# Two graph layers in fp32: the order of the pieces on all engines and on the load queue, written anew

## The chip, the cores and the metric

The kernel runs on one core of a Trainium2 chip. The metric is the time of one execution on the device in microseconds (us); the median of several executions is compared.

## The reference

`x` holds 128 graphs of 128 nodes with 512 features, in fp32. `adj` is one 128 x 128 adjacency matrix for all of them. Two layers follow each other, each with a residual and a layer norm:

```python
# layer 0: attention with 8 heads of 64, masked by adj
q = (x @ Wq + bq).reshape(b, n, H, HD)      # k, v alike
scores = jnp.einsum('bqhd,bkhd->bhqk', q, k) / jnp.sqrt(jnp.float32(HD))
scores = scores + (1.0 - adj)[None, None, :, :] * -1000000000.0
attn = jax.nn.softmax(scores, axis=-1)
out = jnp.einsum('bhqk,bkhd->bqhd', attn, v).reshape(b, n, d)
x = _layernorm(x + out @ Wo + bo)
# layer 1: graph attention, and beta times the node's own product
h = jnp.einsum('bnc,cf->bnf', x, W)
s1 = jnp.einsum('bnf,f->bn', h, a1); s2 = jnp.einsum('bnf,f->bn', h, a2)
e = jax.nn.leaky_relu(s1[:, :, None] + s2[:, None, :], negative_slope=0.2)
e = e * mask[None, :, :]                    # mask is adj
att = jax.nn.softmax(e, axis=2)
x = _layernorm(x + jax.nn.elu(jnp.einsum('bij,bjf->bif', att, h) + beta * h))
```

## The kernel before

**Tiling.** A group is two graphs (64 groups). Each of the five products with a 512 x 512 weight (q, k, v, w for Wo, h for W) is done in 2 x 2 blocks with seven block products instead of eight: some factors are differences of weight blocks (`weight_sum`, made once at the start) or of blocks of the activations (`block_sum`, on GpSimd, POOL). `product` (L318, L325) issues the matmuls of one of the seven; the products of q and k run over two groups at once, those of v, w and h over one. `take_part` (L369, L372, L375) takes a sum out of PSUM and `add_block` (L383, VectorE, DVE) adds a second one to it. The running sums stay in PSUM: `main` and `two` from product 1 or 2 on, `side` from product 7 on, all from one pool of eight banks.

**What happens to a graph.** The blocks of x come in by four DMAs (`load_blocks`, L86), DVE turns them (`turn_x`, L248), POOL makes the block sums. After q and k: `scores` (matmuls psc, L397, two banks), `mask` (DVE, L405, two halves), `row_max` (L413), `exps` (ScalarE, ACT, L419), `row_inv` (L426), `normalise` (ACT, L433). The normalised weights must be transposed in blocks of 32: `attn_write` sends them to DRAM (SP, L440), `attn_read` brings them back block by block with four DMAs (SP, L445), and `turn_attn` turns the blocks on DVE (L462, two halves). Then `attend` (matmuls po, L472), `attend_evict` (ACT, L484), the product w, statistics, and the second layer: row products (L523), logits, softmax (L612 to L641), the weights of which take the same way through DRAM (`weights_write` L587, `weights_read` L594, `weights_turn` L600), `aggregate` (matmuls pz, L660), the product h, ELU (L671 to L680), layer norm and `store` (L750). The tile of raw x for the residual comes in by `fetch_x` (L96).

**What sets the order.** Nothing schedules at run time or at build time: every piece of this work stands in a list with a place, a number in us that is only used to sort. `rows(g)` gives the places for an even and an odd group, `last_rows(g)` those of the last two groups, and a table `other` replaces them for groups 0 to 5 and the groups 58 to 61. `lay(g)` adds `(g // 2) * STEP` to each place, so two groups (four graphs) make one step. About 40 `at(...)` lines place the weight sums and loads. All pieces are sorted by place, and each is issued when its turn comes; so this one order is also the order of instructions on PE (TensorE), DVE, ACT and POOL and of the DMAs on SP, which takes most loads and stores. An engine works strictly in that order, and SP too: a DMA that must wait holds those behind it.

In the steady step of the kernel before, the pieces around the attention of an even group have these places:

```python
(20.282, attn_write, b0), (26.115, attn_read, b0), (28.151, attn_write, b1),
(31.844, turn_attn, b0, 0), (32.855, attn_read, b1), (34.286, turn_attn, b0, 1),
(34.906, turn_attn, b1, 0), (35.094, turn_attn, b1, 1),
(35.392, attend, b0), (35.411, attend, b1),
```

Between the places 28.151 and 32.855 the odd group's two `fetch_x` (29.459 and 31.350) and the `fetch_blocks` of the odd group of the next step (−41.301 in its own step, so 31.323 here) stand on the same queue.

Of the kernel before, what the change touches and what calls it, by code (L numbers as in the profile page):

```python
# [13 lines left out]
P = 128  # L14
# [4 lines left out]
STEP = 72.624  # L19
# [3 lines left out]
def gnn_two_layers(  # L23
# [40 lines left out]
    G = 2  # L64
# [155 lines left out]
    def weight_sum(name, n, eng):  # L220
        w_sb = W_SB[name]
        a11, a21 = w_sb[:, :2, :HF], w_sb[:, :2, HF:]
        a12, a22 = w_sb[:, 2:, :HF], w_sb[:, 2:, HF:]
        if name not in sums:
            sums[name] = cpool.tile([P, 3, G, HF], F32, tag=f"s_{name}", name=f"s_{name}")
        s2, s3, s4 = (sums[name][:, i] for i in range(3))
        if n == 3:
            eng.tensor_tensor(s3, a11, a21, ALU.subtract)
        elif n == 1:
            eng.tensor_tensor(a21, a21, a22, ALU.add)  # L230
        elif n == 2:
            eng.tensor_tensor(s2, a21, a11, ALU.subtract)
        else:
            eng.tensor_tensor(s4, a12, s2, ALU.subtract)
        left[name] = {1: a11, 2: a12, 3: s4, 4: a22, 5: a21, 6: s2, 7: s3}


    right, tx, qT, kT, vb, y, hp, main, side, oT, zT, xr = ({} for _ in range(12))
# [20 lines left out]

    def block_sum(name, g, n):  # L260

        if name == "x":
            b11, b12, b21, b22, (t1, t2, t3, t4) = x_blocks(g % 2)
        else:
            src = oT if name == "w" else zT
            b11, b12 = src[g * G][:, :2], src[g * G + 1][:, :2]
            b21, b22 = src[g * G][:, 2:], src[g * G + 1][:, 2:]
            if (name, g) not in tx:
                tx[name, g] = grp.tile(
                    [P, 4, 2, N], F32, tag=f"t{name}", name=f"t{name}_{g}", bufs=1  # L270
                )
            t1, t2, t3, t4 = (tx[name, g][:, i] for i in range(4))
        to, a, b = {1: (t1, b12, b11), 2: (t2, b22, t1), 3: (t3, b22, b12), 4: (t4, b21, t2)}[n]
        nc.gpsimd.tensor_tensor(to, a, b, ALU.subtract)  # L274
        if name != "x":
            right[name, g] = {1: b11, 2: b21, 3: b22, 4: t4, 5: t1, 6: t2, 7: t3}

    def factor(name, g, n):

        if name in "qkv":  # L280
            b11, b12, b21, b22, (t1, t2, t3, t4) = x_blocks(g % 2 if name == "v" else None)
            return {1: b11, 2: b21, 3: b22, 4: t4, 5: t1, 6: t2, 7: t3}[n]
        if (name, g) in right:
            return right[name, g][n]

        src = oT if name == "w" else zT
        return {1: src[g * G][:, :2], 2: src[g * G][:, 2:]}[n]
# [114 lines left out]
    def mask(b, j):  # L402
        if j == 0:
            s_t[b] = wk2.tile([P, H, N], F32, tag="s", name=f"s_{b}")
# [10 lines left out]
    def exps(b, k):  # L415
        if k == 0:
            rsum[b] = st.tile([P, H], F32, tag="rsum", name=f"rsum_{b}")
# [10 lines left out]
    def normalise(b, k):  # L428

        if k == 0:  # L430
# [27 lines left out]
    def turn_attn(b, half):  # L458
        if half == 0:
# [305 lines left out]
    def rows(g):  # L765

        b0, b1 = g * G, g * G + 1
        if g % 2 == 0:
            return (
                (-63.18, fetch_blocks, g), (-56.066, turn_x, g, 0), (-50.12, turn_x, g, 1),  # L770
                (-32.921, block_sum, "x", g, 3), (-31.465, block_sum, "x", g, 1),
                (-28.542, product, "q", g, 1), (-28.403, take_part, "q", g, 1, 0, 0),
                (-26.676, product, "k", g, 1), (-26.003, product, "k", g, 2),
                (-24.525, product, "q", g, 7), (-23.847, product, "q", g, 2),
                (-22.29, take_part, "k", g, 1, 0, 0), (-22.016, add_block, "q", g, 2, 0, 0),
                (-20.3, block_sum, "x", g, 2), (-19.926, product, "q", g, 6),
                (-17.572, add_block, "k", g, 2, 0, 0), (-16.877, take_part, "q", g, 6, 1, 0),
                (-16.095, fetch_x, b1), (-13.558, product, "k", g, 6), (-12.431, product, "q", g, 5),
                (-11.287, take_part, "k", g, 6, 1, 0), (-11.187, take_part, "q", g, 5, 1, 1),
                (-10.474, product, "k", g, 7), (-9.901, fetch_x, b0), (-9.327, product, "k", g, 5),  # L780
                (-7.731, take_part, "k", g, 5, 1, 1), (-7.172, block_sum, "x", g, 4),
                (-7.022, product, "q", g, 3), (-6.693, add_block, "q", g, 7, 1, 1),
                (-3.761, product, "q", g, 4), (-3.502, add_block, "k", g, 7, 1, 1),
                (-2.536, product, "k", g, 3), (-2.35, product, "k", g, 4),
                (-1.976, add_block, "q", g, 4, 1, 0), (0.256, take_part, "k", g, 3, 0, 1),
                (0.285, take_part, "q", g, 3, 0, 1), (0.542, add_block, "k", g, 4, 1, 0),
                (1.258, scores, b0), (1.278, scores, b1), (2.004, residual, b1),
                (3.445, product, "v", g, 1), (3.721, mask, b0, 0), (4.631, mask, b0, 1),
                (4.957, row_max, b0), (5.077, take_part, "v", g, 1, 0, 0),
                (5.333, product, "v", g, 6), (5.333, exps, b0, 0), (5.499, residual, b0),  # L790
                (6.069, product, "v", g, 7), (6.116, exps, b0, 1), (6.127, mask, b1, 0),
                (6.728, take_part, "v", g, 6, 1, 0), (7.139, exps, b0, 2), (8.211, exps, b0, 3),
                (8.411, product, "v", g, 5), (10.448, mask, b1, 1),
                (11.898, take_part, "v", g, 5, 1, 1), (12.291, row_inv, b0),
                (12.598, normalise, b0, 0), (12.926, product, "v", g, 2), (13.642, normalise, b0, 1),
                (14.582, add_block, "v", g, 7, 1, 1), (14.95, normalise, b0, 2),
                (15.194, row_max, b1), (15.197, normalise, b0, 3), (16.817, exps, b1, 0),
                (17.265, product, "v", g, 4), (17.509, exps, b1, 1),
                (18.686, add_block, "v", g, 2, 0, 0), (19.881, product, "v", g, 3),
                (19.881, exps, b1, 2), (20.282, attn_write, b0), (20.467, exps, b1, 3),  # L800
                (22.18, row_inv, b1), (22.328, add_block, "v", g, 4, 1, 0),
                (22.702, normalise, b1, 0), (22.86, normalise, b1, 1), (26.083, normalise, b1, 2),
                (26.115, attn_read, b0), (26.457, normalise, b1, 3), (28.151, attn_write, b1),
                (29.815, take_part, "v", g, 3, 0, 1), (31.844, turn_attn, b0, 0),
                (32.855, attn_read, b1), (34.286, turn_attn, b0, 1), (34.906, turn_attn, b1, 0),
                (35.094, turn_attn, b1, 1), (35.392, attend, b0), (35.411, attend, b1),
                (38.896, attend_evict, b0), (38.952, attend_evict, b1), (39.488, product, "w", g, 1),
                (40.642, block_sum, "w", g, 1), (44.25, take_part, "w", g, 1, 0, 0),
                (45.185, block_sum, "w", g, 2), (48.299, product, "w", g, 6),
                (48.643, take_part, "w", g, 6, 1, 0), (48.916, block_sum, "w", g, 3),  # L810
                (50.753, product, "w", g, 2), (51.619, product, "w", g, 5),
                (51.848, product, "w", g, 7), (52.53, take_part, "w", g, 5, 1, 1),
                (52.885, block_sum, "w", g, 4), (53.606, add_block, "w", g, 2, 0, 0),
                (54.759, add_block, "w", g, 7, 1, 1), (54.917, product, "w", g, 3),
                (55.177, take_part, "w", g, 3, 0, 1), (55.873, product, "w", g, 4),
                (55.948, bn_stats, y, b1, "c"), (59.19, add_block, "w", g, 4, 1, 0),
                (59.58, row_product, b1, 0), (59.651, bn_aggr, b1, "c"),
                (59.978, bn_stats, y, b0, "c"), (60.733, bn_aggr, b0, "c"),
                (61.568, row_product, b1, 1), (62.033, add_eps, g, "c"), (62.533, inv_std, g, "c"),
                (63.073, row_product, b0, 0), (63.654, row_product, b0, 1), (64.313, scale_s, g),  # L820
                (64.596, s2_turn, g), (65.373, s2_write, g), (66.603, norm_c, b0),
                (72.522, norm_c, b1), (72.851, s2_read, g), (73.73, edge, g, 0),
                (74.467, edge, g, 1), (74.643, leaky, g), (74.812, edge_max, g),
                (77.496, edge_exp, g), (79.435, edge_inv, g), (80.677, weights, g, 0),
# [492 lines left out]
```

## Time and profile before

| | |
|---|---|
| time, median of 3 runs | 2369.22 us (2368.44 to 2373.42) |
| span of the profiled execution | 2365.3 us, TensorE clock 0.998 |
| ACT busy | 1494.1 us (63%) |
| POOL busy | 874.8 us (37%) |
| DMA | 269.31 MB, mean 114 GB/s |

A profile is of one execution; its span runs from the first to the last instruction. Here it is 3.9 us below the median of the runs. A line of a group or of the timeline reads: start or busy us, engine, line, operation, output tile <- input tiles, count, and in brackets the idle time of the engine ahead of it with what ended it. SPq is the queue of SP's own instructions, which issue DMAs; the number beside such a line is the time that issuing took, not the transfer.

The chain of waits, followed back from the last instruction, is made of these engines:

```profile
PE 86%; DMA 6%; DVE 3%; SPq 3%; issue 1%; ACT 1%; DVEq 0%; ACTq 0%; POOLq 0%; POOL 0%
```

### The profile page before, as it was taken

How to read it: one execution, taken by the hardware profiler on the slowest of the kernel's cores; microseconds unless marked ns; L12 is line 12 of the kernel's file. 1: busy time of each engine (PE TensorE's matmuls, PEld its weight loads, DVE VectorE, ACT ScalarE, POOL GpSimd, SP SyncE). 2: the span in 40 equal slices, each digit the busy share in tenths (PEclk: the TensorE clock that was granted, in tenths of full speed). 3: DMA queues.
4: the chain of work that ended last, by engine and by line, in shares of the span. 5: the costliest groups of instructions: out<-in, count | busy, mean ns of one | idle time of the engine just before them, and what ended most of it. 6: DMA issues, size and time to landing. Idle time of an engine off the chain costs nothing.

```text
span 2365.3 us, 42947 instructions
## 1 busy us (share of the span) xinstructions
PE 2332.2 (99%) x14129; PEld 2045.5 (86%) x14129; DVE 1923.8 (81%) x4198; ACT 1494.1 (63%) x5251; POOL 874.8 (37%) x1044
## 2 busy tenths in 40 slices
PE   9999999999999999999999999999999999999997
PEld 8888888888888888888888888888888888888885
DVE  7778887888887888878888887888788887888887
ACT  4565665766756666667566576665666666756665
POOL 6333333343333343433333333333334343333331
PEclk9999999999999999999999999999999999999999
DMA  5433434334334343343343443433434434344332
GB/s 184 123 94 110 128 91 127 109 103 134 97 112 131 99 117 119 97 132 101 111 133 91 120 124 94 130 114 94 136 97 114 124 96 128 101 112 135 92 125 76
DMA packets 255942, 269.31 MB, mean 114 GB/s; under 512 B 57356, under 2 KB 204568, under 8 KB 255336
## 3 DMA queue, kind: packets, MB, share of 16 engines
q1 hardware_dynamic: 254160, 265.06, 38.3%
q8 instruction: 112, 1.84, 0.3%
q14 instruction: 110, 0.90, 0.1%
q10 hardware_dynamic: 1256, 0.66, 0.1%
q0 software_dynamic: 304, 0.85, 0.1%
HBM read 157.62 MB, written 108.85 MB: 113 GB/s over the span
## 4 chain that ended last, share of the span: by engine, by line
PE 86%; DMA 6%; DVE 3%; SPq 3%; issue 1%; ACT 1%; DVEq 0%; ACTq 0%; POOLq 0%; POOL 0%
PE p1w L318 12%; PE p1q L325 9%; PE p1k L325 9%; PE p1v L318 9%; PE p1h L318 8%; PE psc L397 5%; PE pz L660 5%; PE p7q L325 5%; PE p7k L325 5%; DMA ab<-scr 5%; PE p7w L318 4%; PE po L472 4%; PE p7v L318 4%; PE p7h L318 3%; PE p2q L325 2%; PE p2k L325 2%
## 5 line engine op out<-in xcount | busy, mean ns | idle before, releaser
L419 ACT ACTIVATE s<-s,nmax 128x128 f32<-128x128 f32 x1024 | 397.1, 392 | 109.0 <-DVE nmax L413 109.0
L433 ACT ACTIVATE sb<-s,rinv 128x128 f32<-128x128 f32 x1024 | 323.0, 394 | 1.4 <-DMA scr<-sb 1.3
L484 ACT ACTIVATE oT<-po,bias_c 128x128 f32<-128x128 f32 x512 | 145.9, 380 | 222.6 <-PE po L472 222.1
L375 ACT ACTIVATE kT<-p1k,bias_c 128x256 f32<-128x256 f32 x256 | 106.2, 466 | 182.9 <-PE p1k L325 182.9
L372 DVE TENSOR_TENSOR w<-p1w,x 128x256 f32<-128x256 f32 x252 | 105.9, 420 | 140.9 <-PE p1w L318 140.6
L453 POOL TENSOR_TENSOR x<-x,bo_b_in 128x512 f32<-128x512 f32 x128 | 175.6, 1373 | 71.5 <-DMA x<-in_x_dram 71.1
L405 DVE SCALAR_TENSOR_TENSOR s<-psc,amask 128x512 f32<-128x512 f32 x256 | 165.7, 670 | 41.8 <-PE psc L397 40.1
L462 DVE STREAM_TRANSPOSE attnT<-ab 128x512 f32<-128x512 f32 x256 | 169.7, 691 | 34.2 <-DMA ab<-scr 34.2
L419 ACT ACTIVATION_READ_ACCUMULATOR s<-s,nmax 128x1 f32 x1024 | 195.3, 191 | 0.0
L369 ACT COPY h<-p1h 128x256 f32<-128x256 f32 x252 | 94.5, 375 | 157.8 <-PE p1h L318 151.8
L523 DVE SCALAR_TENSOR_TENSOR ya<-w,wa_row 128x512 f32<-128x512 f32 x256 | 191.8, 749 | 2.3
L274 POOL TENSOR_TENSOR tx<-xT 128x256 f32<-128x256 f32 x128 | 92.4, 734 | 188.4 <-DVE xT L248 164.0
L413 DVE TENSOR_REDUCE nmax<-s 128x8 f32<-128x1024 f32 x128 | 155.6, 1216 | 2.3
L274 POOL TENSOR_TENSOR th<-zT 128x256 f32<-128x256 f32 x63 | 46.1, 731 | 273.3 <-ACT zT L667 273.3
L248 DVE STREAM_TRANSPOSE xT<-xblk 128x512 f32<-128x512 f32 x128 | 141.9, 1110 | 5.4 <-DMA xblk<-in_x_dram 5.3
L472 PEld LDWEIGHTS po<-attnT,v 128*64 128x64 f32 x2048 | 109.8, 137 | 38.2 <-DVE attnT L462 15.9
L472 PE MATMUL po<-attnT,v 128*64 128x128 f32 x2048 | 132.3, 277 | 10.1 <-DVE attnT L462 9.9
L660 PEld LDWEIGHTS pz<-attT,x 128*128 128x128 f32 x1024 | 130.5, 193 | 9.8 <-issue 4.9
L369 ACT COPY v<-p1v 128x256 f32<-128x256 f32 x256 | 91.7, 371 | 70.2 <-PE p1v L318 66.1
L660 PE MATMUL pz<-attT,x 128*128 128x128 f32 x1024 | 131.5, 277 | 4.1 <-DVE attT L600 2.7
L318 PE MATMUL p1v<-wv_sb,xT 128*128 128x256 f32 x512 | 133.9, 385 | 0.0
L318 PE MATMUL p1w<-wo_sb,oT 128*128 128x256 f32 x504 | 132.5, 385 | 0.0
(681 smaller groups left out, 6153.3 us busy)
## 6 DMA issues: line engine op xcount, KB each, us to landing
scr<-sb SPq DMA_DIRECT2D x128, 512.0 KB
ab<-scr SPq DMA_DIRECT2D x512, 128.0 KB
x<-in_x_dram SPq DMA_DIRECT2D x128, 256.0 KB
out_dram<-u SPq DMA_DIRECT2D x127, 256.0 KB
xblk<-in_x_dram SPq DMA_DIRECT2D x252, 128.0 KB
pb<-s2d SPq DMA_DIRECT2D x62, 128.0 KB
attd<-att SPq DMA_DIRECT2D x62, 128.0 KB
ab<-attd SPq DMA_DIRECT2D x248, 32.0 KB
```

Source lines behind the costliest of these rows:

```text
L318: nc.tensor.matmul(out, b[:, c, :], a[:, c, :], start=first and c == 0, stop=(c == 1), skip_group_check=True,)
L325: nc.tensor.matmul(out[:, m, :], a[:, c, m * P : (m + 1) * P], b[:, c, :], start=first and m == 0 and c == 0, stop=(c == 1), skip_group_ch ...
L369: nc.scalar.copy(dst, src)
L405: nc.vector.scalar_tensor_tensor(s_t[b][:, j * HP : (j + 1) * HP, :], psc[b][j], SCALE, amask.rearrange("p (o n) -> p o n", o=1).broadcast ...
L413: nc.vector.tensor_reduce(nmax[b], s_t[b], AX.X, ALU.max, negate=True)
L419: nc.scalar.activation(s_t[b][:, h, :], s_t[b][:, h, :], AF.Exp, bias=nmax[b][:, h : h + 1], accum_out=rsum[b][:, h : h + 1],)
L433: nc.scalar.mul(sb[b][:, :, h, :], s_t[b][:, h, :].rearrange("p (b c) -> p b c", c=Q), rinv[b][:, h : h + 1],)
L453: nc.gpsimd.tensor_tensor(xr[b], xr[b], later["bo"], ALU.add)
L462: nc.vector.transpose(attnT[b].rearrange("p h (a r) -> p a h r", r=Q)[:, rows], ab[b].rearrange("p a (h c) -> p a h c", c=Q)[:, rows],)
L472: nc.tensor.matmul(po[b][j * HD : (j + 1) * HD, m, :], vb[b][:, h * HD : (h + 1) * HD], attnT[b][:, j * HP + m, :], start=True, stop=True,)
L523: nc.vector.scalar_tensor_tensor(z, y[b], 1.0, wa_row[j], ALU.mult, ALU.mult, accum_out=s12[g][:, i, j : j + 1])
L660: nc.tensor.matmul(pz[b][:, c, :], x1[b][:, c * P : (c + 1) * P], attT[g][:, i, :], start=True, stop=True,)
```

## The change

All places are new, and `STEP` is 72.19 instead of 72.624. So that any order can be written, three helpers no longer depend on which part comes first: the factors of a product are named by `part` before their block sums are issued, `left` is filled at the head of `weight_sum`, and a tile is allocated by whichever half or part comes first. The number of instructions on each engine, the arithmetic and the tiles are the same.

```diff
-STEP = 72.624
+STEP = 72.19
...
+    def part(name, g, k):
+        i = int(k[1]) - 1
+        if name in "qkvx":
+            b11, b12, b21, b22, t = x_blocks(None if name in "qk" else g % 2)
+            return t[i] if k[0] == "t" else {"b11": b11, "b12": b12, "b21": b21, "b22": b22}[k]
+        if k[0] == "b":
+            src = (oT if name == "w" else zT)[g * G + int(k[2]) - 1]
+            return src[:, 2 * i : 2 * i + 2]
+        if (name, g) not in tx:
+            tx[name, g] = grp.tile([P, 4, 2, N], F32, tag=f"t{name}", name=f"t{name}_{g}", bufs=1)
+        return tx[name, g][:, i]
...
     def factor(name, g, n):
...
+        return part(name, g, ("b11", "b21", "b22", "t4", "t1", "t2", "t3")[n - 1])
...
     def mask(b, j):
-        if j == 0:
+        if b not in s_t:
...
```

The places that matter for the text below, even group, before and after (b0, b1 are its two graphs):

| piece | before | after |
|---|---|---|
| scores b0, b1 | 1.258, 1.278 | 3.373, 2.413 |
| exps b1, first to last | 16.817 to 20.467 | 14.370 to 17.078 |
| attn_write b0, attn_read b0 | 20.282, 26.115 | 14.498, 17.153 |
| attn_write b1 | 28.151 | 20.928 |
| fetch_blocks, fetch_x of other groups between them | yes | no |
| attn_read b1 | 32.855 | 23.583 |
| turn_attn b0, b1 (the earlier half) | 31.844, 34.906 | 23.333, 29.930 |
| attend b0, b1 | 35.392, 35.411 | 32.389, 33.269 |
| product v, 1 and 2 | 3.445, 12.926 | −44.207, −41.618 |

For the odd group of a step:

| piece | before | after |
|---|---|---|
| scores b0, b1 | 35.432, 35.452 | 4.333, 34.289 |
| attn_read b1 | 69.49 | 63.183 |
| turn_attn b1, the earlier half | 71.946 | 67.674 |
| attend b0, b1 | 73.841, 73.861 | 72.703, 73.583 |

At the start, the five constant loads of `load_later` (adjacency, beta, bo, the two halves of a; on POOL's queue) are issued before the first block sums instead of after six of them; the adjacency's even before the operation that makes the identity matrix. TensorE begins with the products 2 and 1 of q and then of k, which need no differences, where it began with 1 and 7 of q. At the end the scores of graphs 126 and 127 stand earlier among the products, in the matmuls' order by some 10 and 5 us.

## The prediction

> **What bounds the kernel now.** I read the page's busy shares first, then the waits of TensorE, then the line of the attention transpose, then one step in the timeline on three engines.
>
> ```profile
> PE 2332.2 (99%) x14129; PEld 2045.5 (86%) x14129; DVE 1923.8 (81%) x4198; ACT 1494.1 (63%) x5251; POOL 874.8 (37%) x1044
> ```
>
> TensorE (PE) is busy for 99% of the span, and the change takes no matmul away. So only gaps between matmuls can be won. The waits of PE say which:
>
> ```profile
> PE po L472 <- DVE attnT L462: 9.9, 18, 1.2
> PE pz L660 <- DVE attT L600: 2.7, 1, 2.7
> PE early L145 <- DMA bias_rows<-in_L_gnn_bv_dram: 2.0, 1, 2.0
> ...
> PE pz L660 <- DVE vec_('c',60)_22068 L512: 1.4, 1, 1.4
> PE p1v L318 <- DVE v L383: 1.2, 1, 1.2
> ```
>
> Total us, times, longest. One wait repeats, the attention product (po) on the transposed weights (attnT); the others happen once, at the start or the end. The line of the transpose itself, L462, says what it waits for and who waits for it:
>
> ```profile
>   DMA ab<-scr: 34.2, 32
> who waited for it (us, times):
>   PEld po L472: 15.9, 25
>   PE po L472: 9.9, 18
> ```
>
> The 32 times are one per step of four graphs. A stalled step, seen on SP (the load queue), DVE and PE:
>
> ```profile
> 1987.81 0.42 SPq L440 DMA_DIRECT2D scr<-sb  x1
> 1990.79 1.75 SPq L445 DMA_DIRECT2D ab<-scr  x4
> 1995.93 0.34 SPq L440 DMA_DIRECT2D scr<-sb  x1
> 1996.70 0.35 SPq L96 DMA_DIRECT2D x<-in_x_dram  x1
> 1997.16 1.98 SPq L86 DMA_DIRECT2D xblk<-in_x_dram  x4
> 1999.25 0.39 SPq L96 DMA_DIRECT2D x<-in_x_dram  x1
> 1999.74 2.97 SPq L445 DMA_DIRECT2D ab<-scr  x4
> ```
>
> ```profile
> 2007.13 1.31 DVE L462 STREAM_TRANSPOSE attnT<-ab 128x512 f32<-128x512 f32 x2 [1.95 <-DMA ab<-scr]
> ```
>
> ```profile
> 2008.49 1.09 PE L472 MATMUL po<-attnT,v 128*64 128x128 f32 x16 [1.15 <-DVE attnT L462]
> ```
>
> The first graph's scores go to DRAM at 1987.81 and are read back from 1990.79. The second graph's are written at 1995.93, but six transfers of the next input stand between its write and its read (1996.70 to 1999.25). The data is there at 2007.13, DVE idle for 1.95 us before it, and PE loses 1.15 us.
>
> What can be won at most: a step holds 14 products of q and k at 1.728 us start to start, 42 of v, w and h at 0.864, and po 3.80, scores 3.98, pz 3.56, together 71.8 us. The best steps take 72.18 (score starts at 883.04 and 955.22 in the timeline), because the small matmuls cost some 0.4 us at their borders, in both orders. The mean of 26 steps is (2210.37 − 319.99) / 26 = 72.71 (starts of pz). So about 0.53 us a step is stall. The span, 2365.3, is 2305.5 us of matmuls at their own spacing, 8.2 before the first product beyond the warm-up's, 2.0 in the first scores (to 66.7), 26.1 to 2226.7 (29.7 steps: 11.3 of borders, about 15 of stalls), 13.4 from there to PE's end at 2355.2, and 10.1 of tail.
>
> **What the Trainium skill says.** "DMA: Bandwidth & Descriptors", section "Queues, rings and completion order": each DMA engine consumes one queue's descriptors in ring order, and goes round between queues packet by packet. The trace agrees: in the step of 1054.74 the 512-byte packets of xblk moved until 1056.3, and the read's 1024-byte packets only from 1057.2 to 1059.8; the first graph's read, issued at 1045.77 with nothing ahead of it, moved from 1046.9 to 1049.2. Its section "Anatomy of one DMA" gives some 2 us of fixed cost, most of it waiting for the write's receipt; here write to read issue is 2.98 us (1987.81 to 1990.79), so that stays in the chain. "TensorE: Matmul & The Clock Gate", "What's actually happening": after an idle window of about 3.4 us the clock halves. One place agrees: after the 2.7 us wait at 2315.98 two pz take 3.48 us, elsewhere 1.78.
>
> **The change, part by part.** No instruction is added or dropped on any engine; all is order.
>
> *Steady step, queue.* Between the second write and read nothing is left on SP (the blocks and x are issued after the read or elsewhere in the step). That removes 1999.74 − 1996.70, about 3.0 us, and the read's data no longer lies behind xblk's packets: about 3.7 us from issue to landing instead of 6.2, 2.5 us more.
>
> *Steady step, compute.* The second graph's scores now come first on PE, and its masks close up. Counted from the start of its scores with before's durations: scores, both masks (0.6 each), maximum (1.14) and the first graph's 8 exponentials (0.39 each) end at 9.9, its 8 normalise (0.30 each) with copies at 13.2, the second's exponentials at 16.6, reciprocal and normalise at 19.6, write 19.7, read 22.6, data 26.5, two transposes of 0.65 end at 27.8. PE's order puts the second attention product at about 31.2. So 3.4 us of cover. If the read were as slow as now (6.2), the end is 30.4 to 31.0 and 0.2 is left. The stall goes in both cases; what is late next is the third score block in a row (below), the ACT copies of h before two products (cover 1.3) and the transposed weights of the second layer (1.4), each off the path by that much. I cost them at nothing, but leave 0.07 us a step for chance meetings of transfers, 2 us in all: **−13 us** of the 15. Range −15 (all) to −4 (copies take 0.35 a step back).
>
> *Moved work.* The v products of the even graphs start a step earlier; their two running sums hold one PSUM bank of eight for 53 planned us (places −44.2 to 8.9; before 3.4 to 19.9). Score blocks need two banks each, and three of them in a row (before: two) make six. This takes no time while DVE empties banks in time: a mask takes 0.6 us, a score block 1.0, and what is ahead of the masks on DVE leaves 1.3 us. Cost 0, bounds 0 to 1.2 a step.
>
> *Start.* POOL issues the five constant loads first (before: at 12.62 to 15.44). They take 0.71 + 0.54 × 2 + 1.06 = 2.85 us of POOL, only the first of them (0.71) ahead of ident, which the warm-up at 1.48 waits for; it ends at 8.1 now and would end at 8.8, still before the first product at 10.21. But their 0.85 MB (queue 0) now run beside wq and xblk, in a stretch where the DMA is full (412 GB/s from 7.00 to 10.20). If they take their whole share, wq comes 0.85 / 0.412 = 2.1 us later, if none, 0: I take +1.2. The stalls at 43.70 (1.24) and 45.97 (0.3) are gone, as the v products no longer wait there: −1.5. The four products that start need 6.9 us, against 7.05 of weight differences and block sums behind wq: +0.2. Sum **0**, bounds ±1.5.
>
> *End.* pz of group 61 waits 2.71 us and then 1.7 us at half clock. DVE was the chain there: adds, maximum and statistics queue ahead of the transpose. The scores of graph 126 move up by 10 us, those of 127 by 5, so their masks and one maximum are out of this stretch; I count 7.4 us of DVE behind the weights where PE leaves 7.0, so 0.5 of the wait stays, without the half clock: −3.9. PE's order behind it is the same, and DVE, which caught up in that pause, now reaches attnT of 126 (0.7) and the spread of the second logits (1.0) late: +1.4 to +1.7. Tail unchanged (10.1). Sum **−2.5**, bounds −6 to +1.
>
> Sum: −13 + 0 − 2.5 = −15.5; the profiled execution goes from 2365.3 to 2349.8. The median of the runs stands 3.9 above that execution (2369.22), so 2353.7; I say 2353.5. A measurement can tell some 0.2%, 4.7 us, from no change.
>
> **Rivals.**
> - *Forecast, steady stalls gone:* 2353.5, own range 2346 to 2361. Chance 0.60.
> - *The stall moves on:* the next late thing (ACT's copies of h, or the transposed weights) takes back 0.35 us a step: −15.5 + 10 = −5.5, 2363.7. For it: ACT's queue is denser around them. Against: covers of 1.3 us and more. Chance 0.16; nearly half of it lies within 0.2%.
> - *The ends are worse:* constants delay wq by 2.1, pz keeps its wait and half clock: −15.5 + 2 + 5 = −8.5, 2360.7. Speaking for it: PE's order at the end is nearly the same. Chance 0.10.
> - *Slower, score blocks waiting for banks:* three in a row with a bank held make PE wait for DVE's masks in each step. If DVE is late by its cover and another block, the price is 1.2 us a step, 31 × 1.2 = 37: 2369.2 − 15.5 + 37 = 2391. From 0.5 us a step it eats the gain (15.5 / 31). For it: PE is 99% busy, so nothing hides such a wait, and DVE at 81% is the next engine. Against: the waits of before show no score block waiting for DVE beyond "issue". Chance 0.14.
>
> Faster by over 0.2%: 0.60 + 0.09 + 0.09 = 0.78; within: 0.07 + 0.01 = 0.08; slower: 0.14. Range 2344 to 2369: it takes in the bounds of the three sums (−15 −1.5 −6 gives 2346.7; a little is left below for borders) and the two rivals that stay faster, and leaves out the slower one.
>
> **What would show it.** Right: the row "po <- attnT" of PE's waits falls from 9.9 to under 2 us; DVE's idle before the transpose under "ab<-scr" nearly goes; mean step 72.2 to 72.3 (pz start to pz start); on SP the second read follows its write by about 3 us; pz of group 61 waits under 1 us with the clock full after it. Wrong: a new repeated wait of PE of 0.3 us or more a step, with psc or p1h as the waiting group, or a first product later than 12.5 us.

## The result and the profile after

| | before | after |
|---|---|---|
| median of the runs | 2370.01 us (2368.44 to 2373.42, 4 runs) | 2394.78 us (2393.06 to 2395.28, 4 runs) |
| span of the profiled execution | 2365.3 us | 2393.4 us |

The ratio after to before is 1.0101, 95% interval 1.0087 to 1.0115: the change makes the kernel slower by 1.0%. TensorE's clock is 0.998 in both.

The page of after, busy time of the engines and the chain that ended last:

```profile
PE 2350.2 (98%) x14129; PEld 2044.6 (85%) x14129; DVE 1945.4 (81%) x4198; ACT 1482.8 (62%) x5251; POOL 875.6 (37%) x1044
...
PE 43%; DVE 17%; ACT 11%; DMA 8%; issue 3%; SPq 2%; POOL 0%; DVEq 0%; POOLq 0%
```

The chain was PE for 86% before and is PE for 43% now; DVE and ACT have 28% of it. Something outside PE paces the kernel, though PE is still busy for 98% of the span. The tile view of the transposed weights (attnT) says that the old stall is gone:

```profile
  DMA ab<-scr: 2.8, 4
...
who waited for it (us, times):
  ACT oT L480: 33.0, 37
```

DVE's idle before this transpose fell from 34.2 to 2.8 us, and PE is no longer among those who wait for it. The waits of PE in after (total us, times, longest) show what came instead:

```profile
PE p1h L314 <- ACT h L365: 13.1, 28, 1.3
PE early L145 <- DMA bias_rows<-in_L_gnn_bv_dram: 5.2, 1, 5.2
```

A product of h waits for ACT to copy a finished sum of h out of PSUM (L365, `take_part`), 28 times. The mean step, from one p2q to the next over 23 steps, is 73.30 us; it was 72.71.

**Where the 28.1 us between the two spans lie.** I put PE's matmuls on an axis of their own spacing, as the prediction did: each takes there the time that such a matmul has from its start to the next one's when nothing is waited for. Then I subtracted that axis from the true starts. What remains is PE's loss, here by stretch of the axis, in us, with the two fastest experiments beside it:

| stretch of PE's axis | before | after | a_pool | b_fetch2 |
|---|---|---|---|---|
| 0 to 60, the start | 10.3 | 15.9 | 13.5 | 11.8 |
| 60 to 400, groups 2 to about 10 | 5.1 | 14.7 | 12.9 | 1.9 |
| 400 to 1990, 22 steady steps | 18.8 | 32.9 | 8.3 | 7.8 |
| 1990 to 2200, late groups | 2.3 | 10.8 | 7.4 | 2.0 |
| 2200 to the last matmul | 12.9 | 4.8 | 4.6 | 11.8 |
| tail behind PE | 10.1 | 8.6 | 8.7 | 10.1 |

The start of a_pool is that of after; the 2.4 between them are the difference of two executions (the wait for bias_rows is 3.3 there and 5.2 in after, and TensorE's granted clock is 0.50 from 13.7 to 17.1 us there and from 14.2 to 21.0 in after). Steady steps cost 14.1 more than before (0.6 a step), the groups on both sides of them 18.1, the start 5.6; the end gives back 9.6.

**One steady step, traced back from PE.** In the timeline of PE in after, the product at 1504.69 starts 1.55 behind the one ahead of it, where 0.86 is the rule, and the one at 1508.51 starts 1.13 behind its own:

```profile
1503.14 1.03 PE L314 MATMUL p7w<-s_w,tw 128*128 128x256 f32 x4
1504.69 1.13 PE L314 MATMUL p1h<-w_sb,th 128*128 128x256 f32 x4 [0.52 <-ACT h L365]
...
1507.38 1.03 PE L314 MATMUL p7v<-s_v,tx 128*128 128x256 f32 x4
1508.51 1.13 PE L314 MATMUL p1h<-s_h,zT 128*128 128x256 f32 x4
```

Together 0.96 us in this step. ACT, in the same stretch:

```profile
1499.96 0.40 ACT L415 ACTIVATE s<-s,nmax 128x128 f32<-128x128 f32 x1 [2.86 <-DVE nmax L409]
...
1503.69 0.69 ACT L429 ACTIVATE sb<-s,rinv 128x128 f32<-128x128 f32 x2 [0.27 <-DVE rinv L422]
1504.29 0.35 ACT L365 COPY h<-p1h 128x256 f32<-128x256 f32 x1
```

The copy is not long (0.35). It stands in ACT's order behind eight exponentials and the first two normalise, and these begin only when the maximum (nmax) is there; ACT idled 2.86 us for it. So the question is why DVE's maximum is late. DVE in after:

```profile
1491.06 0.61 DVE L608 SCALAR_TENSOR_TENSOR ev<-pb,s_in,adj_sb 128x128 f32<-128x128 f32 x2 [1.53 <-DMA pb<-s2d]
...
1493.95 1.07 DVE L734 SCALAR_TENSOR_TENSOR nmr<-mv_f,rstdf_('f',36)_14342 128x2 f32<-128x2 f32 x1
1494.95 1.03 DVE L536 TENSOR_SCALAR x<-w,mv_c,rstdc_('c',38)_14227 128x512 f32<-128x512 f32 x1
1495.90 1.28 DVE L401 SCALAR_TENSOR_TENSOR s<-psc,amask 128x512 f32<-128x512 f32 x2
1497.10 1.70 DVE L637 SCALAR_TENSOR_TENSOR att<-ee,einv,beta_i 128x128 f32<-128x128 f32 x2
1498.72 1.21 DVE L409 TENSOR_REDUCE nmax<-s 128x8 f32<-128x1024 f32 x1
```

and POOL:

```profile
1493.07 0.70 POOL L512 TENSOR_TENSOR rstdf_('f',36)_14342<-vef_('f',36)_14340,mhalf 128x2 f32<-128x2 f32 x1 [4.57 <-DVE vef_('f',36)_14340 L508]
1493.74 1.27 POOL L449 TENSOR_TENSOR x<-x,bo_b_in 128x512 f32<-128x512 f32 x1
1494.96 0.73 POOL L279 TENSOR_TENSOR tw<-oT,oT 128x256 f32<-128x256 f32 x1
...
1497.33 1.32 POOL L449 TENSOR_TENSOR x<-x,bo_b_in 128x512 f32<-128x512 f32 x1
```

nmr works on 128 x 2 elements and takes 1.07 us; with no POOL instruction beside it its median is 0.15. It runs exactly while POOL's residual sum of graph b1 does (1493.74 to 1495.01). Behind that sum POOL's block sum tw (1494.96) lies beside norm_c's x, which takes 1.03 instead of 0.54, and the residual sum of b0 (1497.33) beside the two att, which take 1.70 (1.18 in the profile of a_pool, below). Besides, DVE stands still for 1.53 us before ev, waiting for the spread logits (pb). That wait is new with the change too: in the waits of DVE it has 51.9 us in 41 times in after, and in before it doesn't occur. These were two suspects: POOL's sum beside DVE, and the wait for pb.

### The profile page after: what moved, and what is told of

It reads as the page before. It is cut to its first block, busy times and chain, and to the rows that moved or that the text cites. A ratio compares the mean times of both kernels' runs of the same rounds, so it can differ in the third digit from the quotient of the medians.

```text
span 2393.4 us, 42649 instructions
## 1 busy us (share of the span) xinstructions
PE 2350.2 (98%) x14129; PEld 2044.6 (85%) x14129; DVE 1945.4 (81%) x4198; ACT 1482.8 (62%) x5251; POOL 875.6 (37%) x1044
## 4 chain that ended last, share of the span: by engine, by line
PE 43%; DVE 17%; ACT 11%; DMA 8%; issue 3%; SPq 2%; POOL 0%; DVEq 0%; POOLq 0%
PE p1h L314 6%; PE p1w L314 6%; PE p1v L314 6%; ACT s L415 5%; PE p1k L321 5%; PE p1q L321 4%; ACT sb L429 3%; PE p7h L314 3%; PE p7v L314 3%; PE p7w L314 2%; PE po L468 2%; PE pz L656 2%; DMA xblk<-in_x_dram 2%; PE p7k L321 2%; DMA pb<-s2d 2%
## 5 line engine op out<-in xcount | busy, mean ns | idle before, releaser
L429 ACT ACTIVATE sb<-s,rinv 128x128 f32<-128x128 f32 x1024 | 331.0, 393 | 54.7 <-DVE rinv L422 41.7
L371 ACT ACTIVATE qT<-p1q,bias_c 128x256 f32<-128x256 f32 x256 | 107.2, 471 | 231.0 <-PE p1q L321 230.9
L279 POOL TENSOR_TENSOR th<-zT,zT 128x256 f32<-128x256 f32 x63 | 51.2, 813 | 475.3 <-PE p7h L314 405.6
L365 ACT COPY h<-p1h 128x256 f32<-128x256 f32 x252 | 90.9, 361 | 191.5 <-PE p1v L314 136.5
L519 DVE SCALAR_TENSOR_TENSOR ya<-w,wa_row 128x512 f32<-128x512 f32 x256 | 176.1, 688 | 2.0
L449 POOL TENSOR_TENSOR x<-x,bo_b_in 128x512 f32<-128x512 f32 x128 | 166.5, 1303 | 18.0 <-DMA x<-in_x_dram 18.0
L393 PE MATMUL psc<-kT,qT 64*128 64x128 f32 x2048 | 133.8, 279 | 0.6 <-ACT oT L480 0.5
L314 PE MATMUL p1h<-w_sb,zT 128*128 128x256 f32 x504 | 132.2, 385 | 1.8 <-ACT zT L663 1.5
L279 POOL TENSOR_TENSOR tx<-xT 128x256 f32<-128x256 f32 x128 | 108.5, 849 | 68.8 <-DVE xT L248 67.3
L676 DVE SCALAR_TENSOR_TENSOR u<-h,u 128x512 f32<-128x512 f32 x126 | 127.9, 1016 | 6.6 <-ACT h L667 6.4
L393 PEld LDWEIGHTS psc<-kT,qT 64*128 64x128 f32 x2048 | 120.5, 188 | 13.5 <-issue 11.6
```

What stands on the lines that cost most here:

```text
L279: nc.gpsimd.tensor_tensor(part(name, g, to), part(name, g, a), part(name, g, b), ALU.subtract)
L314: nc.tensor.matmul(out, b[:, c, :], a[:, c, :], start=first and c == 0, stop=(c == 1), skip_group_check=True,)
L371: nc.scalar.activation(dst[:, m, :], src[:, m, :], AF.Identity, bias=BIAS[name][:, 2 * i + m : 2 * i + m + 1],)
L393: nc.tensor.matmul(psc[b][j][:, m, :], qs[feats, m, :], ks[feats, m, :], start=True, stop=True,)
L429: nc.scalar.mul(sb[b][:, :, h, :], s_t[b][:, h, :].rearrange("p (b c) -> p b c", c=Q), rinv[b][:, h : h + 1],)
L449: nc.gpsimd.tensor_tensor(xr[b], xr[b], later["bo"], ALU.add)
```

## The experiments

Each edit is to places in the lists; the first word says to which kernel. Times are medians. The kernel before had 2370.68 beside the first four runs, 2367.97 beside the next four and 2369.40 beside the last two.

**a_pool: after, the odd group's residual sums moved.**

```diff
-(75.2984, residual, b1)
+(56.5, residual, b1)
-(78.6994, residual, b0)
+(79.85, residual, b0)
```

> The changed kernel, with the odd group's two residual additions on POOL (1.3 us each) moved out of the stretch in which DVE masks and finds the maximum (from 75.30 and 78.70 to 56.5 and 79.85). Theory A1 (DVE is late there because POOL runs at the same time: 1.70 us for two of the weights that take 0.70 alone): nmax 1.0 us earlier, PE's waits for h fall from 1.0 to about 0.3 a step, 2394.8 - 15 = 2380 (2374 to 2386). Theory A2 (DVE is late by the wait for pb alone): 2392 to 2396.

Measured: 2365.61, ratio to before 0.9976 (0.9965 to 0.9987), 29.2 below after: theory A1, with a gain twice as large as I had expected (its range ended at 2374). The same operations of DVE, of the same groups, in the profile of a_pool, where they come 20 us sooner:

```profile
1471.01 0.61 DVE L608 SCALAR_TENSOR_TENSOR ev<-pb,s_in,adj_sb 128x128 f32<-128x128 f32 x2 [1.76 <-DMA pb<-s2d]
...
1473.90 0.14 DVE L734 SCALAR_TENSOR_TENSOR nmr<-mv_f,rstdf_('f',36)_14343 128x2 f32<-128x2 f32 x1
1473.95 0.54 DVE L536 TENSOR_SCALAR x<-w,mv_c,rstdc_('c',38)_14228 128x512 f32<-128x512 f32 x1
1474.41 1.28 DVE L401 SCALAR_TENSOR_TENSOR s<-psc,amask 128x512 f32<-128x512 f32 x2
1475.61 1.18 DVE L637 SCALAR_TENSOR_TENSOR att<-ee,einv,beta_i 128x128 f32<-128x128 f32 x2
1476.71 1.21 DVE L409 TENSOR_REDUCE nmax<-s 128x8 f32<-128x1024 f32 x1
```

From the start of ev to the start of nmax it is 5.70 us, against 7.66 in after: 0.93 less for nmr, 0.49 for x, 0.52 for att, which is all of it. The masks, which read PSUM, and the maximum keep their durations. Most steps are 72.16 us, and PE's wait for ACT's copy is a matter of the ends only:

```profile
PE p1h L314 <- ACT h L365: 2.2, 3, 1.3
```

The wait for pb is still there, and longer (1.76); with the collision gone the step has room for it. Taking one POOL instruction of 1.27 us out of this stretch is worth 1.1 us a step. The graph b0's sum is still in it, at 1476.60, but now beside the maximum, which it doesn't lengthen; in after it began beside att (1497.33).

The Trainium skill, "SBUF — State Buffer", section "SBUF: two separate sides", says why these operations and not others: VectorE and GpSimd share one pair of SBUF ports as an exclusive lock, held for a whole instruction by the one that starts first; on VectorE's side an operation with two SBUF inputs (against a GpSimd one that reads SBUF) or in a two-port mode takes it. The trace of the kernel before agrees, and shows both sides of the lock. Its row product ya reads two tensors from SBUF and meets POOL's residual sum in most steps. At 909.97 it starts just ahead of the sum, at 982.14 just behind:

```profile
909.97 0.69 DVE L523 SCALAR_TENSOR_TENSOR ya<-w,wa_row 128x512 f32<-128x512 f32 x1
909.98 1.81 POOL L453 TENSOR_TENSOR x<-x,bo_b_in 128x512 f32<-128x512 f32 x1 [0.25 <-DMA x<-in_x_dram]
...
982.12 1.26 POOL L453 TENSOR_TENSOR x<-x,bo_b_in 128x512 f32<-128x512 f32 x1 [0.21 <-DMA x<-in_x_dram]
982.14 1.79 DVE L523 SCALAR_TENSOR_TENSOR ya<-w,wa_row 128x512 f32<-128x512 f32 x1
```

The one that starts first keeps its time and the other takes some 0.5 to 1.1 us longer. Over the whole run, ya takes 1.75 us where the sum began first (median of 18) and 0.69 where it began second (14); the sum takes 1.27 and 1.75. Operations that read PSUM, and the maximum, are not held: in after, with no POOL instruction beside them and with POOL busy for most of them, masks take 0.68 and 0.68, maxima 1.18 and 1.21. The agreement has limits. x has one tensor input and is held all the same (1.03 against 0.54), which fits the page only if it runs in a two-port mode, and no run here shows that; and in before a small POOL operation on 128 x 2 elements (L516) doesn't hold ya even where it began first (0.69, 31 times).

**a_half: after, only the second of the two moves.**

```diff
-(78.6994, residual, b0)
+(79.85, residual, b0)
```

> The changed kernel, with only the second of the odd group's two residual additions moved (b0, from 78.70 to 79.85), the one that runs on POOL while DVE makes the second layer's weights. Theory A (a sum of delays: the softmax is 3.1 us later than its place, of it 1.5 by the wait for pb, 0.6 by the first residual, 1.0 by the second, and the copies of h have 2.6 us of room): 2.1 us is left, which the room covers, so the step falls to 72.2 and the time to 2366 as with both moved. Theory B (both collisions must go): about half, 2378 to 2388.

Measured: 2391.31, ratio 1.0100 (1.0085 to 1.0115). POOL's order in the steady step stays what it was: the two residual sums run at 1490.09 and 1493.67 there, 3.58 apart, and 3.59 apart in after. So the edit changes nothing there, my expectation of a gain was wrong, and the whole gain of a_pool comes from the first sum, b1.

**a_pb: after, the fetches that share the queue with pb moved.**

```diff
-(69.6814, fetch_x, b0)
+(60.9, fetch_x, b0)
-(-74.2686, fetch_blocks, g)
+(-69.4, fetch_blocks, g)
```

> The changed kernel with both residuals where they are, and the transfers that run beside the read of pb moved (odd b0's x from 69.68 to 60.9, the even group's blocks from -74.27 to -69.4). Theory A (a sum of delays): pb lands 0.9 us sooner, DVE's wait for it falls from 1.5 to 0.6 a step, 2.2 us of lateness is left against 2.6 of room, so the step falls to 72.2 to 72.4 and the time to 2366 to 2372. Theory B (POOL beside DVE is the cause alone): 2390 to 2396, whatever pb does.

Measured: 2384.20, ratio 1.0069 (1.0052 to 1.0086). DVE's wait for pb falls from 51.9 to 40.8 us in all, ev comes 0.4 earlier against the scores, the step is 72.85 (0.45 less). So theory B is wrong: an earlier ev brings the maximum forward by the same 0.4, and the two delays add up ahead of one cover. Theory A took the wait to fall by 0.9 a step, which it did not; the collision stays, and so does most of the loss. What the whole wait for pb is worth was not tested. That the collision alone is enough to lose or to win the step is shown by a_pool, which keeps the wait and loses the stall.

**a_copies2 and a_copies: after, the two copies of h earlier in ACT's order.**

```diff
-(156.4864, take_part, "h", g, 6, 1, 0)
+(155.4, take_part, "h", g, 6, 1, 0)
-(160.4294, take_part, "h", g, 5, 1, 1)
+(159.4, take_part, "h", g, 5, 1, 1)
```

In a_copies the second place is 158.7. There the block of h is taken ahead of its own product 5, so that part of h is another one.

> The changed kernel, with the two copies of h earlier in ACT's order (take_part 6 from 156.49 to 155.4, ahead of the first normalise; take_part 5 from 160.43 to 159.4, two exponentials earlier, after its product). Nothing of DVE, POOL or SP is moved. Theory A (PE loses time only where it waits for these copies): the loss goes though the softmax stays late, 2394.8 - 24 = 2371 (2366 to 2376). Theory B (the late softmax hits PE elsewhere as well): 2380 or more.

> The changed kernel, with two copies of h on ACT moved ahead of what they stand behind (odd group's take_part 6 from 156.49 to 155.4, ahead of the first normalise; take_part 5 from 160.43 to 158.7, ahead of the second graph's exponentials). Theory A (the softmax is late and the copies stand behind it, PE waits for the copies): both waits of p1h on h go, some 1.0 us a step over 26 steps, so 2394.8 - 24 = 2371 (2368 to 2376). Theory B (the whole softmax chain is late and something else of it is as late as the copies): less than half of that, 2384 or more.

Measured: a_copies2 2389.36, ratio 1.0090, as theory B had it; a_copies 2438.69, ratio 1.0278. The second says nothing on the theory, as its edit orders the copy before what it copies. In a_copies2 PE waits for another copy of h instead, 26 times and 13.2 us in all, against 28 times and 13.1. The copies are where the lateness reaches PE; it is not made there.

**b_fetch: before, with fetches moved ahead of the second write.**

```diff
-(-41.301, fetch_blocks, g)
+(-45.8, fetch_blocks, g)
-(29.459, fetch_x, b1)
+(26.5, fetch_x, b1)
-(31.35, fetch_x, b0)
+(26.6, fetch_x, b0)
```

> The kernel before, with one thing of the change alone: from group 6 to 57 the odd group's two x tiles and the next odd group's blocks are issued on SP ahead of the second attention write (places 26.5, 26.6, 26.82) and no longer between it and its read. Theory A (the stall of po on attnT before is the queue position of that read): the row po <- attnT falls from 9.9 us to under 2, the step from 72.71 to 72.2 to 72.3, so about 2370 - 12 = 2358 (2355 to 2361). Theory B (the read was hidden anyway, and another wait of the order takes the place at once): 2366 to 2371.

Measured: 2440.91, ratio 1.0295 (1.0273 to 1.0318), far off. The queue of SP in b_fetch:

```profile
1087.51 4.18 SPq L96 DMA_DIRECT2D x<-in_x_dram  x2
1091.75 1.90 SPq L86 DMA_DIRECT2D xblk<-in_x_dram  x4
1093.75 0.40 SPq L440 DMA_DIRECT2D scr<-sb  x1
```

The two issues of x stretch over 4.18 us here, though issuing one takes 0.35 to 0.37: SP stands still between them, and the write of the weights stands behind them. The waits of SP in b_fetch name DVE, in a row that has only 1.1 us in before:

```profile
SPq L96 <- DVE mv_c L498: 89.2, 27, 3.8
```

This fits a buffer of x that is not free yet: the last addition on DVE that reads a tile of x starts at 1090.9 and takes 0.42, and the second issue comes at 1091.3. The old stall grows from 9.9 to 65.8 us. I had looked at the order of the queue and not at when the buffers come free.

**b_fetch2: before, with the same fetches behind the second read.**

```diff
-(-41.301, fetch_blocks, g)
+(-39.3, fetch_blocks, g)
-(29.459, fetch_x, b1)
+(33.1, fetch_x, b1)
-(30.188, residual, b1)
+(36.0, residual, b1)
-(31.35, fetch_x, b0)
+(33.2, fetch_x, b0)
-(32.03, residual, b0)
+(37.5, residual, b0)
```

> The kernel before, with the odd group's x tiles and blocks issued behind the second attention read (33.1, 33.2, 33.32) and the two residuals after them (36.0, 37.5); the earlier form of this put them ahead of the write, where they waited for their buffers and held the write. Theory A (the second read's place in the queue is what stalls po in the kernel before): read some 3 us earlier and nothing ahead of its packets, po's wait from 9.9 to under 2 us, step 72.2 to 72.3, 2370 - 12 = 2358 (2355 to 2361). Theory B (what is moved comes too late for turn_x and the block sums, or collides anew): 2366 or more.

Measured: **2351.97**, ratio 0.9932 (0.9917 to 0.9947), faster than both kernels and 3 us below the range of theory A. SP's queue in b_fetch2:

```profile
1984.52 0.34 SPq L440 DMA_DIRECT2D scr<-sb  x1
1987.16 1.73 SPq L445 DMA_DIRECT2D ab<-scr  x4
1988.99 0.84 SPq L96 DMA_DIRECT2D x<-in_x_dram  x2
```

The second read follows its write by 2.64 us and the fetches follow the read. Nearly every step is 72.16 to 72.17, and PE's wait for attnT is 0.5 us in all. The edit moves two residual sums of POOL beside the three fetches, so it isn't the queue alone by its form. But DVE's idle time before these transposes, in which it waits for the data of the read, falls from 34.2 to 2.8 us; the stall was the read's. Five places do what the prediction's first term promised from the change, without its second half.

**b_start: before, with only the constants' load put first, as the change has it.**

```diff
-at(7.564, load_later)
+at(-75.7, load_later)
```

> The kernel before with one part of the change alone: the constants' load at the head of the start (7.564 becomes -75.7). My theory, that the software queue's packets take every second turn from the weights of the first products: the first product comes at 14 to 15 us instead of 10.2, DVE's s_q waits for wq, and the time rises by 4.7 to 7.6 us less the start's waits for the constants (1.7 us) that go: 2371 to 2376. Rival, that the first weights would be late only by the change's other moves: the first product comes by 11.5 us and the time is 2366 to 2370.

Measured: 2375.38, ratio 1.0023 (1.0012 to 1.0034); its span is 7.6 above that of before. Its PE at the start:

```profile
14.07 3.44 PE L325 MATMUL p1q<-xT,wq_sb 128*128 128x256 f32 x8 [1.69 <-DMA wq_sb<-in_L_gnn_Wq_dram]
17.35 1.89 PE L325 MATMUL p7q<-tx,s_q 128*128 128x256 f32 x8
```

The first product comes at 14.07 instead of 10.21 and takes 3.44 instead of 1.99; the granted clock is 0.55 from 14.0 to 17.4. This is within what I had expected. This one line of the change costs the kernel before some 6 us (0.12 to 0.34% by the interval).

**a_start: after, the constants' load put back behind the first weights.**

```diff
-at(-75.7299, load_later)
+at(-26.1, load_later)
```

> The changed kernel, with the five constant loads issued behind five block sums of x, as in the kernel before, and not ahead of the identity. Theory A (the software queue's packets took half of the DMA engines' turns from wq, and the clock halved in the wait): first product at 10.2 to 11 instead of 14.95, no half clock, 2394.8 - 7 = 2388 (2386 to 2390). Theory B (the later start is absorbed, because the first steps wait for other loads): 2392 to 2395.

Measured: 2394.86, ratio 1.0098 (1.0082 to 1.0115), no gain, as theory B had it. The first product does come at 10.28 with a full clock, but DVE then waits for beta, and s_q, on which PE waits 4.4 us, stands behind it:

```profile
23.67 2.27 DVE L176 TENSOR_SCALAR beta_i<-ident,beta_b_in 128x128 f32<-128x128 f32 x1 [6.36 <-DMA beta_b_in<-in_L_gnn_beta_dram]
```

**a_start2: after, with a_pool's moves, the constants' load put back, and beta put behind the weights.**

```diff
-at(-75.7299, load_later)
+at(-26.1, load_later)
-at(14.6145, weight_sum, "q", 4, nc.vector)
+at(0.25, weight_sum, "q", 4, nc.vector)
-at(-5.5068, make_beta)
+at(20.65, make_beta)
```

> The changed kernel with its first residual sum moved as in a_pool (2365.6 us there), and beside it its start undone in full: the constants' load behind the first weights, the table of betas behind them at 20.65, and the sum s_q 4 ahead of it. My theory: the late constants cost the start 4.7 us of waiting and about 2.9 us of half clock, and what a_start took back was DVE waiting for beta with s_q 4, s_k 4 and the weights' columns behind it. So the first product comes at 10.3 us, no wait of more than 2 us follows, and the time is 3 to 7 us below a_pool: 2359 to 2362. Rival: the columns and biases that need the constants come late in any order, PE waits for them inside the first 40 us, and the time stays at 2364 to 2366.

Measured: 2365.39, ratio 0.9983 (0.9976 to 0.9990), as a_pool; the rival was right. The first product comes at 10.26, and DVE waits for the next constant:

```profile
28.61 0.94 DVE L185 SCALAR_TENSOR_TENSOR wa_t<-w_sb,uf_in 128x512 f32<-128x512 f32 x1 [8.92 <-DMA uf_in<-in_L_gnn_a_dram]
```

PE's lead over a_pool on its axis is 5.2 us at 15 and 0.05 at 30. In the order of after DVE needs all the constants within its first 30 us, so their 0.85 MB are paid for early or late. Moving DVE's uses of them too was not tried.

## Why the prediction was wrong

It said 2353.5 with 0.78 for faster; measured were 2394.78. Two of its own signs of being wrong came: a repeated wait with p1h as the waiting group, and a first product later than 12.5 us (14.95).

*Steady step, queue: right.* The stall on attnT went, as forecast, and nothing is left on SP between the second write (1506.69 in after) and read (1509.32). b_fetch2, on the kernel before, loses 14.5 us less from 60 to 2200 of the axis (16.0 in the medians), where the term was −13.

*Steady step, compute: this step failed.* The prediction named the next late thing, "the ACT copies of h before two products (cover 1.3)", and "cost them at nothing". The chain ahead of the copies was summed from durations of before: scores, masks, maximum and the first graph's eight exponentials should end 9.9 us after the scores start, so the exponentials, eight times 0.39, should begin at 6.8. Median over the steps is 8.3 in after and 6.9 in a_pool. So the total was right for a DVE without the collision, though partly by luck: the parts that it names (a score block of 1.0, two masks, the maximum, eight exponentials) come to some 6.5 of its 9.9, and it doesn't name the wait for pb, which is part of a_pool's 6.9. What it left out is that the change puts a residual sum of POOL (1.27 us) into this stretch, which lies beside nmr and moves POOL's next sums to where x and att run; the three take 1.9 us more. Counted from the scores' start, the copy of h ends at 13.1 in the step shown, and PE needs it at 12.5; in a_pool it ends at 11.4. The true cover is 1.05, and 1.7 was laid upon it. Over the 22 steps this is 24.6 us (32.9 − 8.3), 1.1 a step. Without it, in a_pool, these 22 steps give 10.5 us (18.8 − 8.3), 0.48 a step, where the forecast had 13 for 31 steps, 0.42 a step. The collision is the largest part of the miss and not the whole: a_pool, without it, still stands 12 us above the forecast, above all by the start and the groups beside the steady part (both below).

*The second rival* had the right place and the wrong price: it took ACT's copies of h to take back 0.35 a step, and left the sum on the faster side. From 0.48 a step, which is what the removed stall was worth here (10.5 / 22), the sign turns.

*Moved work, PSUM banks: right.* Among the longest waits of after the third score block in a row does not appear as a wait for DVE's masks; the fourth rival's mechanism, that score blocks wait, is not the one that made the kernel slower. That its 2391 lies near the measured time is chance.

*Start: mis-sized.* The forecast was 0 ± 1.5: wq late by 1.2, stalls of 1.5 gone. The stalls went (−2.1 to axis 60), but the first product is 4.7 late, and then the clock is low (0.50 granted from 14.2 to 21.0):

```profile
14.95 3.76 PE L321 MATMUL p2q<-xT,wq_sb 128*128 128x256 f32 x8
18.50 3.14 PE L321 MATMUL p1q<-xT,wq_sb 128*128 128x256 f32 x8
21.48 1.89 PE L321 MATMUL p2k<-xT,wk_sb 128*128 128x256 f32 x8
```

From 14.95 to 21.48 are two blocks of products at 3.55 and 2.98 instead of 1.73 each, 3.1 us more. The third block starts at 21.48 where it starts at 13.77 in before: start and clock together +7.7. The upper bound of the delay was taken as the constants' bytes at the full rate of the DMA, 2.1 us; b_start shows the delay without the rest of the change, 3.9 us. The DMA view of 7 to 9 us (packets, MB, share of the 16 engines) shows how much the constants (q0) take from the weights (q1), in before

```profile
q1 hardware_dynamic: 110, 0.81, 97.9%
```

and in after

```profile
q0 software_dynamic: 76, 0.23, 36.2%
q1 hardware_dynamic: 40, 0.30, 36.0%
```

The two queues have equal shares, as they would by taking turns. Turns are not all of the delay: from 5 to 7 us q1 moves 0.43 MB in before and 0.16 in after, though q0 moves only 0.01 there. What holds q1 back in that stretch stays open. In after the warm-up's first operation is also 1.05 later (2.53 against 1.48), behind the constants' issue on POOL, where the prediction had 0.71.

The clock depends on the execution as well. The prediction cites an idle window of some 3.4 us and calls the one place in before an agreement, but the pause there is 2.71 (granted clock 0.57 from 2316 to 2320). Shorter ones do it too: b_fetch2, whose start is that of before, has a pause of 2.42 and then 0.50 from 11.2 to 14.6, where the profile of before has a pause of 1.99 and the full clock. So part of the 3.1 us is chance.

*Groups beside the steady part: not looked at.* The prediction treated 60 to 400 and 1990 to 2200 as steady steps. They lose 18.1 us more than before, of which a_pool takes back 5.3. The rest, 12.8, is spread over single delays of more than ten kinds (the longest waits 1.3 and 1.5 us); what causes them was not tested and stays open.

*End: right in kind, too small.* pz of group 61 starts without a wait (2346.92 in the timeline of PE) and its sixteen matmuls take 2.02, so the 2.71 of waiting and the 1.7 of half clock are gone. Gone too are single waits of before that the prediction had not counted (pz at 2250.84 for 1.44, p1w at 2309.57 and 2311.31 for 0.85 and 0.61, p1h at 2341.74 for 0.95). One later piece is late, as forecast (pat waits 1.09 for att at 2376.69). To the last matmul this gives −8.1, and the tail, forecast unchanged, is 1.5 shorter: −9.6 where −2.5 was forecast.

## What to carry to other kernels

When a change moves work in time, list for each stretch on the critical chain what runs beside it on the other engines afterwards, and give a VectorE operation that reads two tensors from SBUF the time that it takes when a GpSimd operation has started ahead of it, not its mean. A cover of 1 us is no cover until every duration in the chain ahead of it is taken under those conditions. Where a stall has one plain cause, as six transfers between a write and a read, move these alone before planning everything anew.

## What the hardware showed that I had not expected

A GpSimd sum of 1.27 us stretched a VectorE operation on 128 x 2 elements from 0.14 to 1.07 us, and left those that read PSUM as they were. Which of the two engines loses is settled by who starts first: in the two pairs shown, 0.01 or 0.02 us apart, ya takes 0.69 or 1.79 us and the sum 1.81 or 1.26. A load of 0.85 MB on the software queue, issued at the head of the program, delayed the first weights by 3.9 us (b_start), nearly twice its size at the DMA's full rate, and the pause of the warmed TensorE then cost slow products on top: 1.4 us in b_start (17.35 − 14.07 instead of 12.05 − 10.21), 3.1 us in after.
